# Unread TensorE products at the seams of a five-stage kernel, with three smaller edits beside them

## The chip, the cores and the metric

The kernel runs on one core of a Trainium2 chip. Its time is the device time of one execution in microseconds (us). Three runs of the kernel before are given, and one further execution was recorded by the profiler; every line of a profile below comes from that one.

## What is computed

The input x has 256 x 256 positions with 32 channels, in fp32. Four layers follow one another, and each adds its result to x:

```python
x = x + attention(_gn(x), ...)   # layer norm over channels, gate, values, projection
x = x + sobel(_gn(x))            # 3x3 mean, two 3x3 derivatives, sqrt(gx*gx + gy*gy + 1e-6)
x = x + sobel(_gn(x))
x = x + recurrence(_gn(x), ...)  # two recurrent layers, 256 steps, 256 sequences
```

`_gn` is a group norm: mean and variance over all positions, for 16 groups of two channels. In the attention the softmax runs over an axis of length one, so the values are merely multiplied by a sigmoid gate and projected. The recurrence has H = 128 hidden units, a normalisation of the four gates in each step, and biases and input weights that the kernel folds together with the last group norm ahead of the first step.

## The kernel before

The whole of x stays in SBUF as a tile of 128 partitions (four positions of one axis by 32 channels) by 64 blocks of 256 columns: `xa`, and a second one, `xb`. A pair is two blocks, 128 x 512; there are NST = 32 pairs. The engines run their own instruction queues in program order, and semaphores tie them together. Five stages follow one another:

1. Load (L163 to L184): x arrives by DMA, TensorE transposes it into PSUM, ScalarE copies it to `xa` (L183), VectorE takes statistics of each pair (L184).
2. Layer norm (L201 to L264). TensorE forms `pc`, the pairs with the group norm applied and their channel mean taken away (L238); ScalarE squares them, VectorE copies them to `xb`; TensorE gathers the variances into `pvar` (L228). ScalarE takes a root of `pvar` (L248), VectorE its reciprocal `rstd` (L249). Then for each pair TensorE spreads `rstd` over the channels into `pb` (L254, 32 rows of the array), VectorE multiplies `xb` by it (L261), and POOL applies `gamma4` and `beta4` (L262). `avg` and `spread`, constants that stage 2 needs, are made by POOL at its head (L204 to L213), when the load stage's SBUF has been released.
3. Attention (L268 to L332), in an order written out by hand. For each pair there are eight gate products `pg` and eight value products `pv` (L279, 32 rows each), sigmoids on ScalarE (L294), VectorE's products `o` (L297), a projection by sixteen matmuls (L303), whose result ScalarE moves out as `r` (L311); POOL adds it to `xa` (L313) and VectorE takes statistics (L316).
4. Sobel, twice (`sobel_layer`). A list of parts with due times, sorted, gives the order. Per pair, ScalarE normalizes the source twice, as `xp` and `xn` (L376); VectorE makes sums `u`, `pp`, `v`; POOL makes the two operands `dh` (L405) and `sh` (L401). TensorE applies the vertical part to them by centre and edge products (L412 or L422, and L452) into `pg1` and `pg0`. ScalarE squares (L458), VectorE adds (`ss`, L462), ScalarE takes the root (L466), VectorE adds the result to the source (L469) and takes statistics (L472). After each statistics part one entry of a list `between` is run. In Sobel 1 it holds the centring of the recurrent weights; in Sobel 2 it is empty.
5. Recurrence (`recurrence`), 256 steps by a plan with due times. The step's chain leads from the gate products `zz` (L763, L788, L793) over squares (L801), sums (L806), a power on POOL (L809), sigmoids and tanh to the new hidden state.

Between stages stands the group norm's seam. `group_norm` aggregates the statistics (`mv`, L139), averages over the group with a TensorE product of one column (`pm`, L141), forms the group variance on VectorE (`mean`, `d`, `q`), averages it with a second product (`pv`, L149), takes a root on ScalarE (`std`, L151), and makes `scale` and `bias`:

```python
nc.tensor.matmul(pm, lhsT=kt[:, K_GN, :], rhs=mv[:, 0:1], start=True, stop=True)
...
nc.vector.scalar_tensor_tensor(q, d, d, mv[:, 1:2], ALU.mult, ALU.add)
...
nc.scalar.activation(std, pv, AF.Sqrt, bias=gn_eps)
```

These steps wait for one another, so the engines are nearly idle there. In the text below seam 1 is the one between load and layer norm, seam 2 the middle of the layer norm (root and reciprocal) with its end, and seams 3, 4 and 5 stand before Sobel 1, Sobel 2 and the recurrence.

In the trace ScalarE has five ACT_TABLE_LOADs of 1283 ns: before the first copy of the load stage, before the first Sqrt (seam 1), before the first Sigmoid (attention), before the next Sqrt (seam 3) and before the next Sigmoid (recurrence). Each stands just ahead of the operation that needs it; Identity, copies and squares have none of their own.

`RecurrentWeights.products` (L607) forms, at seam 4, products of the recurrent weights: a transpose (`pl`), two products `pf` that VectorE adds to the biases `bc` (L617), and one, `pe`, that ScalarE copies in four pieces into `e4` (L625). `RecurrentWeights.finish` (L628) follows at seam 5; it writes `sb` from the group norm's result, forms two products `pg` with it (L641), which ScalarE copies to `fx`, and two small ones, `pk`. `RecurrentInputs` loads the inputs `xt` of the steps by DMA from `xa` and sets their rows of ones by POOL (L680).

Of the kernel before, what the change touches and what calls it, by code (L numbers as in the profile page):

```python
# [16 lines left out]
S = 256  # L17
T = 256
C = 32
# [39 lines left out]
def net_kernel(  # L59
# [71 lines left out]
    NST = NB // 2  # L131

# [3 lines left out]
    def group_norm(stats, psum):  # L136

        mv = small.tile([P, nc.vector.BN_AGGR_DIM], F32, name="mv")
        nc.vector.bn_aggr(mv, stats)  # L139
        pm = psum.tile([P, 1], F32, name="pm", tag="pm", bufs=1)  # L140
        nc.tensor.matmul(pm, lhsT=kt[:, K_GN, :], rhs=mv[:, 0:1], start=True, stop=True)  # L141
        mean = small.tile([P, 1], F32, name="mean")
        nc.vector.tensor_copy(mean, pm)
        d = small.tile([P, 1], F32, name="d")
        nc.vector.tensor_sub(d, mv[:, 0:1], mean)
        q = small.tile([P, 1], F32, name="q")
        nc.vector.scalar_tensor_tensor(q, d, d, mv[:, 1:2], ALU.mult, ALU.add)
        pv = psum.tile([P, 1], F32, name="pv", tag="pm", bufs=1)
        nc.tensor.matmul(pv, lhsT=kt[:, K_GN, :], rhs=q, start=True, stop=True)  # L149
        std = small.tile([P, 1], F32, name="std")  # L150
        nc.scalar.activation(std, pv, AF.Sqrt, bias=gn_eps)  # L151
        scale = small.tile([P, 1], F32, name="scale")
        nc.vector.reciprocal(scale, std)
        bias = small.tile([P, 1], F32, name="bias")
        nc.vector.scalar_tensor_tensor(bias, mean, -1.0, scale, ALU.mult, ALU.mult)
        return scale, bias

# [5 lines left out]
    with tc.tile_pool(name="nat", bufs=3) as natp, tc.tile_pool(  # L163
# [21 lines left out]
        gn = group_norm(stats, ps_in)  # L185
# [9 lines left out]
    KS = NST // 4  # L195
# [5 lines left out]
    with tc.tile_pool(name="ln", bufs=4) as lnp:  # L201


        avg = lnp.tile([P, KS, KS, J], F32, name="avg", bufs=1)  # L204
        nc.gpsimd.memset(avg, 0.0)
        for ks in range(KS):
            nc.gpsimd.tensor_copy(avg[:, ks, ks, :], kt[:, K_AVG, 0:P:C])
        spread = lnp.tile([P, KS * J, C], F32, name="spread", bufs=1)
        for g in range(4):
            rows = slice(g * C, (g + 1) * C)  # L210
            nc.gpsimd.tensor_copy(
                spread[rows], ident[rows, rows].unsqueeze(2).to_broadcast([C, KS * J, C])
            )  # L213
        rstd = lnp.tile([P, 2 * S], F32, name="rstd", bufs=1)
        with tc.tile_pool(name="ps_ln", bufs=6, space=PSUM) as ps_ln, tc.tile_pool(
# [32 lines left out]
            nc.scalar.activation(std, pvar, AF.Sqrt, bias=ln_eps)  # L248
            nc.vector.reciprocal(rstd, std)  # L249
        with tc.tile_pool(name="ps_sp", bufs=8, space=PSUM) as ps_sp:  # L250
            for k, g, ks in pairs:
                rows = slice(g * C, (g + 1) * C)
                pb = ps_sp.tile([P, 2 * S], F32, name="pb")
                nc.tensor.matmul(  # L254
                    pb,
                    lhsT=spread[rows, ks * J : (ks + 1) * J, :].rearrange("p j c -> p (j c)"),
                    rhs=rstd[rows, :],
                    start=True,
                    stop=True,
                )  # L260
                nc.vector.tensor_mul(pair(xb, k), pair(xb, k), pb)  # L261
                nc.gpsimd.tensor_scalar(  # L262
                    pair(xb, k), pair(xb, k), gamma4, beta4, ALU.mult, ALU.add
                )  # L264
# [4 lines left out]
    with tc.tile_pool(name="at", bufs=3) as atp, tc.tile_pool(  # L269
# [48 lines left out]
        with tc.manual_schedule():  # L318
            together((), [(0, j) for j in range(J)])
            together((), [(1, j) for j in range(2)])  # L320
            for i in range(NST):
# [5 lines left out]
                if i >= 1:  # L327
                    project(i - 1)
            for i in range(NST - 1, NST):
# [5 lines left out]
    with tc.tile_pool(name="ps_gn", bufs=1, space=PSUM) as ps_gn:  # L335
        gn = group_norm(stats, ps_gn)
# [8 lines left out]
    def sobel_layer(src, dst, scale, bias, between):  # L345
# [152 lines left out]
        with tc.manual_schedule():  # L498
            for _, k, part, args in todo:
                part(k, *args)  # L500
                if part is statistics and between:
                    between.pop(0)()
# [4 lines left out]
    with tc.tile_pool(name="ps_n", bufs=1, space=PSUM) as ps_n:  # L507
        gn = group_norm(stats, ps_n)
        rw.products(ps_n)
    stats = sobel_layer(xb, xa, *gn, [])  # L510
# [8 lines left out]
    with tc.tile_pool(name="ps_n", bufs=1, space=PSUM) as ps_n:  # L519
        gn = group_norm(stats, ps_n)  # L520
        weights = rw.finish(lw, ps_n, gn)
    with tc.If(plain > 0) as arms:
# [28 lines left out]
class RecurrentWeights:  # L551
# [31 lines left out]
    def centring(self):  # L583
# [21 lines left out]
        return [lambda p=out[i : i + 2]: [f() for f in p] for i in range(0, len(out), 2)]  # L605

    def products(self, psum):  # L607
        nc = self.nc
        pl = psum.tile([P, KX], F32, name="pl")
        nc.tensor.transpose(pl, self.lat, self.ident[:KX, :KX])  # L610
        nc.scalar.copy(self.latt, pl)
        for dst, src in ((self.lat4, self.latt[:, 0:C]), (self.wout4, self.wout)):
            nc.gpsimd.tensor_copy(dst, src.unsqueeze(1).to_broadcast([P, J, C]))
        for l in range(L):
            pf = psum.tile([KX, G], F32, name="pf", bufs=2)
# [3 lines left out]
        pe = psum.tile([P, C], F32, name="pe")  # L619
        nc.tensor.matmul(  # L620
            pe, lhsT=self.lat4.rearrange("p j c -> p (j c)"), rhs=self.wout, start=True, stop=True
        )
        for j in range(J):
            rows = slice(j * C, (j + 1) * C)
            nc.scalar.copy(self.e4[rows, rows], pe[rows, :])  # L625
        nc.gpsimd.tensor_add(self.e4, self.e4, self.ident)
# [31 lines left out]
class RecurrentInputs:  # L658
# [5 lines left out]
    def __init__(self, tc, ctx, xa):  # L664
# [12 lines left out]
        for i in range(self.NX):  # L677
            xt = kp.tile([P, self.XT, J, S], F32, name=f"xt{i}")
            for p in (0, X1):
                nc.gpsimd.memset(xt[p + C : p + KX], 1.0)  # L680
            self.xts.append(xt)
        for k in range(self.NX):
            self.load(k)

# [274 lines left out]
```

## Time and profile before

| | us |
|---|---|
| median of three runs | 2894.18 |
| the runs | 2893.24, 2903.16, 2894.18 |
| the profiled execution | 2892.63 |
| its span | 2890.8 |

| stretch of the profiled execution | us |
|---|---|
| load, up to its last statistics | 0 to 34.6 |
| seam 1, up to the first `pc` | 34.6 to 41.4 |
| layer norm, variances | 41.4 to 79.7 |
| seam 2 and spreading, up to the first `pg` | 79.7 to 105.4 |
| attention | 105.4 to 329.7 |
| seam 3, up to the first product of Sobel 1 | 329.7 to 339.4 |
| Sobel 1 | 339.4 to 480.5 |
| seam 4, up to the first product of Sobel 2 | 480.5 to 490.6 |
| Sobel 2 | 490.6 to 626.9 |
| seam 5, up to the first `zz` | 626.9 to 636.0 |
| recurrence | 636.0 to 2890.8 |

PE is TensorE's matmul queue and PEld its weight loads, DVE is VectorE, ACT ScalarE, POOL GpSimd, SP SyncE. One fp32 matmul appears as two passes, two rows of the trace. A timeline line gives start, duration, engine, line, operation, output<-inputs, shapes, and in brackets the idle time of the engine before it and what ended it. PEclk is the granted share of TensorE's clock. A line on waits gives the sum in us, how often, and the longest.

### The profile page before, as it was taken

To read this page: it belongs to the slowest core of one execution; us is meant where nothing else is said; L and a number is where in the kernel's file an instruction comes from. 1 tells how busy PE (TensorE), PEld (TensorE's weight loads), DVE (VectorE), ACT (ScalarE), POOL (GpSimd) and SP (SyncE) were. 2 spreads that over 40 slices of the span, in tenths; PEclk is the share of its full clock that TensorE was granted. 3 is DMA by queue.
4 is the path that set the end of the run, shared out by engine and by line. 5 is a ranking of instruction groups with operands and counts; after the bars stand their busy time and mean duration, and the time that the engine had idled before them with its cause. 6 is when DMAs were issued, how large, how long until landed. Compare 5 with 4: busy or idle time off the path is not lost.

```text
span 2890.8 us, 40872 instructions
## 1 busy us (share of the span) xinstructions
PE 2754.4 (95%) x9561; PEld 993.9 (34%) x9561; DVE 2422.5 (84%) x6507; ACT 2274.8 (79%) x6961; POOL 1934.2 (67%) x2586
## 2 busy tenths in 40 slices
PE   7899898989999999999999999999999999999997
PEld 4433333333333333333333333333333333333332
DVE  6788798978888888888888888888888888888886
ACT  5477676758888888888888888888888888888886
POOL 2311375657777777777777777777777777777775
PEclk9899999989999999999999999999999999999999
DMA  3000000000000000000000000000000000000000
GB/s 133 1 1 1 16 1 1 1 22 6 16 13 12 12 12 12 12 12 12 12 12 14 12 12 12 12 12 12 12 12 12 12 12 12 13 13 16 7 5 7
DMA packets 94354, 38.53 MB, mean 13 GB/s; under 512 B 74852, under 2 KB 91269, under 8 KB 94104
## 3 DMA queue, kind: packets, MB, share of 16 engines
q1 hardware_dynamic: 93156, 34.67, 5.3%
q8 instruction: 79, 1.29, 0.2%
q14 instruction: 171, 1.40, 0.2%
q10 hardware_dynamic: 148, 0.86, 0.1%
q0 software_dynamic: 800, 0.30, 0.0%
HBM read 10.63 MB, written 8.39 MB: 7 GB/s over the span
## 4 chain that ended last, share of the span: by engine, by line
PE 44%; DVE 32%; POOL 12%; issue 7%; ACT 2%; POOLq 0%; DVEq 0%; ACTq 0%
DVE ve L806 14%; POOL rs L809 11%; PE zz L793 11%; DVE c L852 7%; PE zz L788 6%; PE zz L763 5%; DVE zn L773 4%; PE pv L279 4%; PE pg L452 4%; PE pg L412 3%; DVE c L844 3%; PE pt L864 3%; PE pg L303 2%; PE px L883 2%; PE pg L279 1%
## 5 line engine op out<-in xcount | busy, mean ns | idle before, releaser
L809 POOL TENSOR_TENSOR rs<-ve,mhalf 128x4 f32<-128x4 f32 x1024 | 1040.3, 1016 | 252.0 <-DVE ve L806 225.5
L793 PE MATMUL zz<-wc,hT 128*128 128x512 f32 x2040 | 962.2, 594 | 1.2 <-DVE hT L869 1.2
L801 ACT ACTIVATE sq<-zz 128x512 f32<-128x512 f32 x1024 | 605.4, 591 | 245.7 <-PE zz L793 240.3
L806 DVE TENSOR_REDUCE ve<-sq 128x4 f32<-128x516 f32 x1024 | 694.4, 678 | 9.9 <-ACT sq L801 9.5
L848 POOL TENSOR_TENSOR fc<-ga,c 128x128 f32<-128x128 f32 x1020 | 464.8, 456 | 333.4 <-ACT ga L837 313.3
L782 ACT ACTIVATE ga<-zz,rs 128x128 f32<-128x128 f32 x2048 | 585.0, 371 | 4.6 <-POOL rs L809 1.1
L763 PE MATMUL zz<-fx,xt 33*128 33x512 f32 x2048 | 585.2, 643 | 3.3 <-issue 1.9
L788 PE MATMUL zz<-wc,hT 128*128 128x512 f32 x1024 | 525.3, 595 | 0.0
L793 PEld LDWEIGHTS zz<-wc,hT 128*128 128x128 f32 x2040 | 361.0, 197 | 262.6 <-DVE hT L869 201.6
L844 DVE TENSOR_TENSOR c<-ga 128x128 f32<-128x128 f32 x1024 | 307.5, 300 | 156.3 <-ACT ga L782 98.3
L773 DVE TENSOR_TENSOR zn<-zz,rs 128x256 f32<-128x256 f32 x1024 | 386.2, 419 | 54.8 <-POOL rs L809 20.4
L864 PEld LDWEIGHTS pt<-ident,h 128*128 128x128 f32 x1024 | 142.3, 139 | 797.9 <-DVE h L859 748.9
L864 PE MATMUL pt<-ident,h 128*128 128x128 f32 x1024 | 323.7, 316 | 67.4 <-DVE h L859 40.8
L856 ACT ACTIVATE th<-c 128x128 f32<-128x128 f32 x1024 | 310.4, 303 | 79.6 <-DVE c L852 59.8
L852 DVE TENSOR_TENSOR c<-c,fc 128x128 f32<-128x128 f32 x1020 | 368.8, 362 | 3.1 <-POOL fc L848 2.0
L859 DVE TENSOR_TENSOR h<-ga,th 128x128 f32<-128x128 f32 x1024 | 290.2, 283 | 0.8 <-ACT th L856 0.8
L763 PEld LDWEIGHTS zz<-fx,xt 33*128 33x128 f32 x2048 | 156.6, 185 | 348.2 <-PE zz L793 309.0
L869 DVE COPY hT<-pt 128x128 f32<-128x128 f32 x512 | 147.5, 288 | 111.5 <-PE pt L864 111.5
L837 ACT ACTIVATE ga<-zn 128x256 f32<-128x256 f32 x512 | 208.7, 408 | 3.9 <-DVE zn L773 3.9
L297 DVE TENSOR_TENSOR o<-pv,sg 128x512 f32<-128x512 f32 x256 | 158.0, 679 | 46.5 <-PE pg L279 37.7
L874 POOL TENSOR_TENSOR hs<-hT,hT 128x256 f32<-128x256 f32 x256 | 186.0, 726 | 1.7 <-ACT hT L869 1.7
L788 PEld LDWEIGHTS zz<-wc,hT 128*128 128x128 f32 x1024 | 183.3, 219 | 2.3 <-issue 2.3
(143 smaller groups left out, 2745.6 us busy)
## 6 DMA issues: line engine op xcount, KB each, us to landing
xt<-xa SPq DMA_DIRECT2D x256, 64.0 KB, 2.0
nat<-in_x_dram SPq DMA_DIRECT2D x16, 512.0 KB, 7.1
out_dram<-st SPq DMA_DIRECT2D x256, 32.0 KB, 1.7
wc<-in_L_conv_W_cell_dram SPq DMA_DIRECT2D x2, 512.0 KB, 4.5
kt<-in_consts_dram ACTq DMA_DIRECT2D x1, 832.0 KB, 5.9
wv<-in_L_conv_Wv_dram POOLq DMA_DIRECT2D x4, 32.0 KB, 5.0
wg<-in_L_conv_Wg_dram POOLq DMA_DIRECT2D x4, 32.0 KB, 6.0
gamma<-in_L_conv_ln_gamma_dram POOLq DMA_DIRECT2D x4, 0.1 KB, 6.3
```

What stands on the lines that cost most here:

```text
L763: nc.tensor.matmul(zz, lhsT=x, rhs=fx[rows, l, :], start=True, stop=l == 0 and t == 0)
L773: nc.vector.tensor_mul(four(get("zn"))[:, g, :], four(get("zz"))[:, g, :], get("rs")[:, g].unsqueeze(2).to_broadcast([P, 2, H]),)
L782: nc.scalar.activation(gates(get("ga"), g), gates(x, g), func, scale=scale)
L788: nc.tensor.matmul(get("zz"), lhsT=v["hT", 0, t][:, seqs], rhs=wc[:, l, 0, :], start=False, stop=t == 0)
L793: nc.tensor.matmul(get("zz"), lhsT=v["hT", l, t - 1][:, seqs], rhs=wc[:, l, 1, :], start=False, stop=True,)
L801: nc.scalar.activation(sqs[l, h][:, :, 0:H], four(get("zz")), AF.Square, scale=float(H**-0.5))
L806: nc.vector.tensor_reduce(ve, sqs[l, h], AX.X, ALU.add)
L809: nc.gpsimd.tensor_tensor(rs, get("ve"), inputs.mhalf, ALU.pow)
L844: nc.vector.tensor_mul(c, gates(get("ga"), 0), gates(get("ga"), 3))
L848: nc.gpsimd.tensor_mul(fc, gates(get("ga"), 1), get("c"))
L852: nc.vector.tensor_add(c, c, get("fc"))
L864: nc.tensor.transpose(pt[:, 0:P], get("h"), ident)
```

## The change

Five things are done. `busy` puts unread products (the identity by a 256-column slice, written to a PSUM tile that nobody reads) on TensorE: in `group_norm` before `pm`, two between `pm` and `pv`, and some after `pv`; nine behind the layer norm's root; ten behind the last `pb`. `table` puts a one-element activation of a given function ahead of the place that needs it, so that the table is loaded there. Every second pair of `gamma4`/`beta4` goes from POOL to ScalarE. The weight products move from seam 4 into the `between` list of Sobel 2, where they write to a buffer of `pg1`. POOL's copies for `avg` and `spread` move ahead of the load stage, and POOL's rows of ones behind `finish` in the program.

What the queues hold after it: the products before `pm` stand behind the last ScalarE copy of L183 (seam 1), the last `r` of L311 (seam 3), or the last residual of L469 (seams 4 and 5). The nine wait for the root of L248, the ten for the multiplication of the 25th pair in L261. The Sqrt table of seam 3 is loaded between the last two `r`. In `finish`, `pg` now stands before `pk`. POOL's rows of ones stand at the same place of its queue as before, and no DMA moves on its queue. In the recurrence's steps each engine's instructions and their order are the same, but for the table load ahead of the first sigmoid.

```diff
+    def table(func, after):
+        t = small.tile([P, 1], F32, name="table")
+        nc.scalar.activation(t, after, func, scale=0.0, bias=one)
+
+    def busy(psum, n, rhs=None):
+        junk = psum.tile([P, S], F32, name="junk", tag="junk", bufs=1)
+        for _ in range(n):
+            nc.tensor.matmul(
+                junk, lhsT=ident, rhs=kt[:, 0:2, :] if rhs is None else rhs, start=True, stop=True
+            )
...
-    def group_norm(stats, psum):
+    def group_norm(stats, psum, before, after, rhs=None):
         nc.vector.bn_aggr(mv, stats)
+        busy(psum, before, rhs)
         pm = psum.tile([P, 1], F32, name="pm", tag="pm", bufs=1)
         nc.tensor.matmul(pm, lhsT=kt[:, K_GN, :], rhs=mv[:, 0:1], start=True, stop=True)
+        busy(psum, 2, rhs)
...
         nc.tensor.matmul(pv, lhsT=kt[:, K_GN, :], rhs=q, start=True, stop=True)
+        busy(psum, after, rhs)
...
-        gn = group_norm(stats, ps_in)
+        table(AF.Sqrt, xa[:, NB - 1, 0:1])
+        gn = group_norm(stats, ps_in, 3, 2, xa[:, NB - 1, :])
...
             nc.scalar.activation(std, pvar, AF.Sqrt, bias=ln_eps)
+            table(AF.Sigmoid, std[:, 0:1])
             nc.vector.reciprocal(rstd, std)
+            for _ in range(9):
+                nc.tensor.matmul(
+                    pvar[:, 0:S], lhsT=ident, rhs=kt[:, 0:2, :], start=True, stop=True
+                )
...
-                nc.gpsimd.tensor_scalar(
-                    pair(xb, k), pair(xb, k), gamma4, beta4, ALU.mult, ALU.add
+                if i % 2:
+                    nc.scalar.activation(
+                        pair(xb, k), pair(xb, k), AF.Identity, scale=gamma4, bias=beta4
+                    )
+                else:
+                    nc.gpsimd.tensor_scalar(
+                        pair(xb, k), pair(xb, k), gamma4, beta4, ALU.mult, ALU.add
+                    )
+            junk = ps_sp.tile([P, 2 * S], F32, name="pb")
+            for _ in range(10):
+                nc.tensor.matmul(
+                    junk[:, 0:S], lhsT=ident, rhs=kt[:, 0:2, :], start=True, stop=True
                 )
...
                     project(i - 1)
+            table(AF.Sqrt, one)
             for i in range(NST - 1, NST):
                 project(i)
...
-        gn = group_norm(stats, ps_gn)
+        gn = group_norm(stats, ps_gn, 7, 12)
...
                 if part is statistics and between:
-                    between.pop(0)()
+                    between.pop(0)(lambda: flat(ps_s.tile([P, 2, S], F32, name="pg1")))
...
-        gn = group_norm(stats, ps_n)
-        rw.products(ps_n)
-    stats = sobel_layer(xb, xa, *gn, [])
+        gn = group_norm(stats, ps_n, 6, 12)
+    stats = sobel_layer(xb, xa, *gn, rw.products())
...
-        gn = group_norm(stats, ps_n)
+        gn = group_norm(stats, ps_n, 9, 3)
+        table(AF.Sigmoid, gn[0])
         weights = rw.finish(lw, ps_n, gn)
+        inputs.ones()
...
+        def turn(ps):
+            pl = ps()[:, 0:KX]
+            nc.tensor.transpose(pl, self.lat, self.ident[:KX, :KX])
+            nc.scalar.copy(self.latt, pl)
...
+        def biases(ps, l):
+            pf = ps()[0:KX, :]
             nc.tensor.matmul(pf, lhsT=self.latt, rhs=self.wc[:, l, 0, :], start=True, stop=True)
             nc.vector.tensor_add(self.bc[:, l, :], self.bc[:, l, :], pf)
...
+        return [
+            turn,
+            repeat,
+            lambda ps: biases(ps, 0),
+            lambda ps: biases(ps, 1),
+            output,
+        ]
```

The lines of `avg` and `spread` move unchanged from the layer norm to a place ahead of the load stage, into the pool of constants. `repeat` holds POOL's two broadcast copies, and `output` the product `pe` with its four copies and POOL's addition.

## The prediction

> **What bounds the kernel now.** (Lines are those of the kernel before.) I read the page first, then the stretches between the clock's changes, then the timeline at each seam between stages.
>
> ```profile
> span 2890.8 us, 40872 instructions
> ...
> PEclk9899999989999999999999999999999999999999
> ...
> PE 44%; DVE 32%; POOL 12%; issue 7%; ACT 2%; POOLq 0%; DVEq 0%; ACTq 0%
> ```
>
> The recurrence fills the span from 636 us on, about 8.7 us for each of 256 steps, at full clock. The instructions of its steps, and their order on every engine, stay as they are, so it prices at 0, and what can be won lies in the first 650 us. There the granted clock drops in places. By stretches (us, then busy us of PE, PEld, DVE, ACT, POOL, the clock, DMA):
>
> ```profile
> 37.69:44.52 6.83, 4.27 (x8) 2.52 (x9) 1.46 (x6) 2.23 (x3) 0.39 (x1) 0.50 0.01 1
> 78.65:82.07 3.42, 1.06 (x12) 0.15 (x5) 2.21 (x2) 0.69 (x1) 0.00 (x0) 1.00 0.00 0
> 82.07:88.89 6.82, 4.88 (x22) 2.73 (x24) 4.66 (x6) 0.00 (x0) 1.88 (x3) 0.50 0.00 1
> 92.31:95.72 3.41, 3.41 (x13) 1.68 (x12) 3.41 (x7) 0.00 (x0) 3.41 (x5) 1.00 0.00 0
> 95.72:116.20 20.48, 15.74 (x57) 10.76 (x58) 12.10 (x21) 6.60 (x11) 15.27 (x21) 0.50 0.00 1
> 331.24:344.89 13.65, 6.11 (x18) 3.80 (x18) 7.51 (x14) 6.50 (x11) 7.08 (x7) 0.50 0.18 66
> 474.60:478.01 3.41, 2.30 (x11) 0.64 (x9) 1.92 (x4) 1.87 (x3) 0.14 (x2) 1.00 0.00 0
> 478.01:481.43 3.42, 1.26 (x3) 0.28 (x3) 2.60 (x4) 0.88 (x2) 0.29 (x1) 1.00 0.00 0
> 481.43:495.08 13.65, 7.91 (x19) 4.64 (x21) 8.64 (x17) 5.90 (x14) 6.54 (x6) 0.50 0.00 0
> 628.20:652.09 23.89, 18.94 (x29) 6.66 (x30) 7.93 (x27) 7.66 (x18) 9.54 (x8) 0.50 0.19 47
> 652.09:2860.00 2207.91, 2146.87 (x6711) 749.72 (x6710) 1893.43 (x5641) 1836.10 (x6149) 1645.14 (x2280) 1.00 0.06 12
> ```
>
> Six half-clock spells, all multiples of 3.41 us. A stretch of 3.41 us with TensorE 31% or 37% busy (78.65, 478.01) is followed by a drop, one with 67% (474.60) is not. The 32-row products of L254 lose the clock although PE looks full (92.31).
>
> **The Trainium skill.** "TensorE: Matmul & The Clock Gate", section on the HAM clock gate: a free-running 3.4 us window halves the clock after an idle window and restores it after a busy one. The trace agrees in length and in ratio: weight loads of successive 512-wide passes start 0.43 us apart at 75 us and 0.85 at 43 us. "ScalarE: Activation LUTs", "What ACT_TABLE_LOAD costs", gives 1283 ns for a load, and a drain beside it; the trace has 1283 ns and no drain (std starts 0.01 us after). "SBUF — State Buffer", "Who interferes with whom": a VectorE operation with two SBUF inputs and a GpSimd one that reads SBUF block each other. That is d and q here, behind POOL's copies of L211 (0.68 and 1.05 us; 0.16 and 0.22 at the next seam, where no copy runs):
>
> ```profile
> 36.32 0.68 DVE L145 TENSOR_TENSOR d<-mv,mean 128x1 f32<-128x1 f32 x1
> 37.03 1.05 DVE L147 SCALAR_TENSOR_TENSOR q<-d,mv 128x1 f32<-128x1 f32 x1
> ...
> 38.82 1.28 ACT L151 ACT_TABLE_LOAD   x1 [5.26 <-PE pv L149]
> 40.11 0.26 ACT L151 ACTIVATE std<-pv,gn_eps 128x1 f32<-128x1 f32 x1
> ```
>
> **Price of one unread product.** 128x256 in fp32 is two passes of half the width above: 0.43 us at full clock, 0.85 at half. TensorE keeps its order, so a product delays all that stands behind it.
>
> **Seam 1 (load to layer norm).** The POOL copies move up to about 20 us, so q takes 0.22 and pv could start at 36.8 instead of 38.14. The two products behind pm (35.70) hold PE to about 36.95: pv 1.2 us earlier. The table load (1.28) now runs behind the last copy of L183, at 33.6. From pv at 36.95, std at 37.4, bias by 38.1; the two products behind pv end then too, so pcb starts at 38.15 and the first pc at 38.6 instead of 41.42: 2.8 us. Three products from 33.6 and these four make 3.0 us of work in 5 us, about half of each window, above the 37% that lost the clock, so I take it as held: the pc stream then lacks 3.1 us at half clock, worth 1.55. It is the chain to 79.7 (PE full, DVE 24 of 38 us). **-4.3**; -1.5 if the clock still drops.
>
> **Seam 2 (inside the layer norm).** (Times of before; what seam 1 gave comes off all of them.) Nine products from 80.6 end at 84.5 (3.9 us) and their result is waited for; the reciprocal ends at 83.95, so pb starts 0.65 later than now (84.01), but at full clock: first result 1.05 us after it instead of 2.09. Net -0.4. Then VectorE alone sets the pace, 32 x 0.60 us, to 104.9. POOL's half of gamma/beta on ACT (16 x 0.80, the row of L376) fits into that; POOL ended at 110.99, but nobody waited for its last tiles: 0. The ten products need the bank of the 25th pair, free at 100.65. The clock will have dropped again by then (L254's stream fell to half at 95.7). At 0.85 until one full window passes (about 3.9 us on average), then 0.43: done at 106.9. pg, which waits for that and for VectorE, starts at 107.0 instead of 105.44: **+1.6**. What follows it is shorter:
>
> ```profile
> 107.56 1.28 ACT L294 ACT_TABLE_LOAD   x1 [26.99 <-PE pg L279]
> ...
> 113.39 2.48 DVE L297 TENSOR_TENSOR o<-pv,sg 128x512 f32<-128x512 f32 x4 [8.05 <-PE pv L279]
> ```
>
> From pg to the first o were 7.95 us. Without the table load, with four pg done in 1.1, a sigmoid (0.6), the next two pg and a pv at full clock, about 3.4: o at 110.4, -3.0. VectorE then waits once more for 0.75 (after four o, PE still at half clock), of which I count half: **-3.4**; -5.5 with the ten at full clock, -1 with all ten at half.
>
> **Seam 3 (attention to Sobel 1).** The Sqrt table (1.28 + 0.26) is put between the last two r of L311, where ACT is idle for only 1.1 us: r, POOL's add and the statistics come 0.45 later. It saves 1.3 behind pv. Seven products from 328.1 end at 331.1, before mv (331.2). The two behind pm delay pv by 0.2; pv itself is 0.25 shorter. xp starts 0.9 earlier. Twelve products then fill 5.2 us, up to dh (338.4). The gap before the first is 1.4 us, so the clock holds, and the first two pairs take half. VectorE, full in Sobel, had this wait:
>
> ```profile
> DVE ss L462 <- ACT sq L458: 3.0, 1, 3.0
> ```
>
> It shrinks to 1.1, since POOL's sh and dh (1.0 us each) then lead: with the 0.9, **-2.8**; -3.5 if it goes further, +1 if the clock drops.
>
> **Seam 4 (Sobel 1 to 2).** The weight products leave: pf stood before pv (1.1 us), the four e copies before xp (0.5). But the six products wait for the last residual of L469 (479.78) and take 2.6 us at full clock, and mv is ready at 481.6. PE idles 2.95 us before them, so in about two cases of three a window empties and they run partly at half: 4.2 us. pm comes 0.9 or 2.5 late, xp 0.9 early or 0.6 late. The start of Sobel 2 at full clock gives 1.5 either way. Mean **-1.5**, from -2.4 to +1. The products move into Sobel 2, where VectorE has no idle time: two additions of 0.67 us, **+1.3**; ACT, POOL and PE have room there. A held pg1 bank may cost up to 1.5 more, and half may hide: 0.5 to 3.
>
> **Seam 5 (Sobel 2 to recurrence).** The same, with nine:
>
> ```profile
> 625.44 0.69 DVE L469 TENSOR_TENSOR xa<-xb,pg 128x512 f32<-128x512 f32 x1 [0.76 <-ACT pg L466]
> ...
> 626.89 1.02 DVE L139 BATCH_NORM_AGGREGATE mv<-stats 128x2 f32<-128x192 f32 x1
> 628.05 0.43 PE L141 MATMUL pm<-mv,kt 128*128 128x1 f32 x2 [4.81 <-DVE mv L139]
> ```
>
> From 626.2 they last 3.9 to 5.5 us: pm at 630.1 to 631.7, **2.0 to 3.6 late**. Then three products behind pv are over before VectorE has sb. The two pg at full clock take 1.7 instead of 3.7 us, and pk follows instead of leading: first zz at 635.8 to 637.4 (636.00). Its own passes give 1.0 back. The table load was hidden under L809 and is hidden again. The first products have 33 rows, so the clock drops again soon after. POOL's ones keep their place in its queue; no DMA on SP or POOL's queue moves: 0. About **-0.1**, from -2.5 to +2.5.
>
> **Sum.** -4.3 - 3.4 - 2.8 - 1.5 + 1.3 - 0.1 = -10.8 us. The profiled execution took 2892.6 (span 2890.8 and 1.8 around it), which becomes 2881.8; the median of the runs lies 1.6 above it: **2883.4 us**.
>
> **Rivals.** (a) The clock is held at every seam, the ten products and seams 4 and 5 included: -4.3 - 5.5 - 3.5 - 2.4 + 0.5 - 2.5 = -17.7, 2876.5. Against it: L254's stream, and 2.95 us of idle PE before seams 4 and 5. (b) The products give back what they win: pm late in seams 4 and 5, the ten before pg, bank stalls in Sobel 2, and only table loads, POOL's copies and part of the clock remain: -1.5 - 2 - 1.8 + 1 + 2 + 1 = -1.3, 2893. For it: three of five groups start too late to end before their release. (c) Slower: unread products do not hold or lift the clock, so that the change does not do what it says, and they stand in the way at 0.85 us. Seam 2: 9 and 10 of them put pg 8.5 later, less the table 7.2. Seam 3: pm 3.1 late, pv another 1.3, and twelve more end 7.8 after dh was ready before. Seam 4: 7.4 and 1.3. Seam 5: 8. Total +31, 2925; it decides for slower once three of these four seams run so. Against it: a stream of L238 lifted the clock at 44.5.
>
> **Numbers.** 0.5% is 14.5 us, about what a measurement of this kernel can tell from no change. The forecast 0.60, (a) 0.15, (b) 0.20, (c) 0.05. Past -14.5 lie two thirds of (a) and a twelfth of the forecast (its better ends together): faster 0.15, slower 0.05, same 0.80. The range runs from the edge of (a), 2876, to (b), 2893; left out are (c), half of (b) and a tail of (a).
>
> **What will tell.** Right: full clock from 14 us to about 92, and through 331 to 345; no table load behind any pv; the first o about 29.8 us behind the start of the reciprocal (32.8 now); mv to pm longer at seams 4 and 5 than the 0.06 and 0.14 us now. Wrong: half clock during the twelve products, a wait on VectorE inside Sobel 2, or a step of the recurrence that is not 8.7 us.

## The result and the profile after

| | before | after |
|---|---|---|
| median of 13 runs, us | 2895.58 | 2891.75 |
| lowest to highest, us | 2893.24 to 2903.16 | 2885.46 to 2897.56 |
| profiled execution (span), us | 2892.63 (2890.8) | 2886.19 (2884.4) |

The ratio of after to before is 0.9982 [0.9973, 0.9992]: 0.2% faster, where 10.8 us (0.37%) were forecast. The medians differ by 3.8 us, the profiled executions by 6.4.

The page of the kernel after answers to the three lines shown of before:

```profile
span 2884.4 us, 41191 instructions
...
PEclk9999999999999999999999999999999999999998
...
DVE 32%; PE 26%; POOL 12%; issue 7%; ACT 2%; POOLq 0%; DVEq 0%; ACTq 0%
```

Up to the end of the recurrence the clock's tenths show no dip any more. The 8 in the last slice is the end of the recurrence: its last steps run at half clock, here from 2869.8 us on (14.6 us), in the kernel before from 2877.6 us on (13.3 us). In the last chain TensorE's share is 26% instead of 44%, with VectorE and POOL as before. That is no gain: this chain can be followed back only to 630.4 us, inside the recurrence, that of before to 41.4 us, through all stages, so it says nothing of the seams. The stretches between the clock's changes are the view that matters (us, then busy us of PE, PEld, DVE, ACT, POOL, the clock, DMA share, GB/s):

```profile
23.08:26.49 3.41, 3.37 (x17) 2.96 (x16) 2.50 (x4) 2.34 (x4) 0.99 (x1) 0.50 1.04 396
36.00:42.80 6.80, 6.11 (x23) 3.87 (x23) 3.28 (x10) 2.29 (x5) 0.00 (x0) 1.00 0.00 1
84.53:87.94 3.41, 3.41 (x13) 1.62 (x12) 3.41 (x7) 2.26 (x4) 2.22 (x3) 1.00 0.01 2
87.94:101.59 13.65, 13.65 (x40) 10.11 (x39) 13.65 (x23) 9.19 (x12) 8.86 (x12) 0.50 0.00 1
331.40:345.00 13.60, 13.36 (x48) 5.25 (x46) 10.81 (x17) 8.42 (x16) 9.99 (x8) 1.00 0.00 1
627.23:630.65 3.42, 2.59 (x9) 1.19 (x8) 0.52 (x3) 1.18 (x2) 0.00 (x0) 1.00 0.48 108
630.65:644.31 13.66, 10.19 (x14) 2.91 (x14) 6.42 (x17) 4.39 (x13) 3.67 (x5) 0.50 0.03 6
644.31:2860.00 2215.69, 2153.00 (x6733) 750.59 (x6733) 1901.51 (x5657) 1843.85 (x6167) 1650.80 (x2286) 1.00 0.06 11
```

Three half-clock spells ahead of the recurrence's steady part where before had six, 30.7 us instead of 85.3 in all. Seam 1 and the start of Sobel 1 run at full clock. The 32-row products of the spreading still lose the clock (84.53, then 13.65 at half), and so do the first products of the recurrence.

By stages, worked out from the start and end times in each trace. The half-clock spells ahead of the last steps all last a multiple of 3.41 us, so the clock is taken to change at the edges of windows of that length; the phase is where these edges fall in the kernel. "Other phase" is the profile of experiment E14, which has the same instructions as the kernel after up to the start of the recurrence, but met the clock's windows at other places. "End of attention" is from VectorE's last `o` to `mv`. "Load" runs to the first `mv`; it varied by 34.4 to 36.2 us over all the profiles, with no order by kernel.

| stage | before, us | after, us | difference | forecast | other phase, difference |
|---|---|---|---|---|---|
| load | 34.63 | 35.60 | +1.0 | 0 | 0.0 |
| seam 1 and variances | 45.08 | 40.64 | -4.4 | -4.3 | -4.4 |
| root, spreading, attention | 245.27 | 243.41 | -1.9 | -3.4 | -0.7 |
| end of attention, seam 3, Sobel 1 | 155.55 | 152.88 | -2.7 | -2.8 | -1.0 |
| seam 4 to the first `ss` of Sobel 2 | 16.73 | 14.20 | -2.5 | -1.5 | -1.0 |
| Sobel 2 | 129.61 | 132.40 | +2.8 | +1.3 | +2.8 |
| seam 5 to the first `zz` | 9.11 | 9.22 | +0.1 | -0.1 | +1.8 |
| recurrence | 2254.84 | 2256.04 | +1.2 | 0 | +0.5 |
| sum | 2890.84 | 2884.40 | -6.4 | -10.8 | -2.0 |

Seam 1 in the timeline of the kernel after (start, duration, engine, line, operation; the line numbers are those of each run's own kernel):

```profile
34.61 1.28 ACT L137 ACT_TABLE_LOAD   x1
...
37.29 0.16 DVE L161 TENSOR_TENSOR d<-mv,mean 128x1 f32<-128x1 f32 x1
37.48 0.22 DVE L163 SCALAR_TENSOR_TENSOR q<-d,mv 128x1 f32<-128x1 f32 x1
...
38.18 0.26 ACT L168 ACTIVATE std<-pv,gn_eps 128x1 f32<-128x1 f32 x1 [1.98 <-PE pv L165]
```

`d` and `q` take 0.16 and 0.22 us instead of 0.68 and 1.05, as the copies no longer run beside them (POOL is idle from 36.00 to 42.80), and the table load is over before `pv`. This seam went as forecast.

Between spreading and attention it did not. L296 holds the ten products, L313 `pg`, L328 the sigmoid, L331 `o`:

```profile
99.54 5.28 PE L296 MATMUL pb<-kt,ident 128*128 128x256 f32 x19
...
104.92 1.14 PE L313 MATMUL pg<-xb,wg 32*128 32x512 f32 x8
106.11 3.04 ACT L328 ACTIVATE sg<-pg 128x512 f32<-128x512 f32 x6 [3.58 <-PE pg L313]
...
108.84 4.28 DVE L331 TENSOR_TENSOR o<-pv,sg 128x512 f32<-128x512 f32 x7 [7.15 <-PE pv L313]
```

VectorE's last multiplication ends at 101.68; `pg` starts 3.2 us later, behind the ten. VectorE idles 7.15 us instead of 8.05.

VectorE's waits inside Sobel 1 and then inside Sobel 2 (sum, how often, longest):

```profile
DVE ss L497 <- ACT sq L493: 1.2, 1, 1.2
```

```profile
DVE u L418 <- ACT xn L411: 1.9, 3, 0.7
```

The wait at the start of Sobel 1 fell from 3.0 to 1.2. In Sobel 2, `u` waits three times for `xn`. Before it did so once:

```profile
DVE u L383 <- ACT xn L376: 0.7, 1, 0.7
```

Seam 5, from the last residual (L504) over the unread products (L143) to `pm`:

```profile
617.69 0.69 DVE L504 TENSOR_TENSOR xa<-xb,pg 128x512 f32<-128x512 f32 x1 [0.76 <-ACT pg L501]
...
618.52 4.12 PE L143 MATMUL junk<-kt,ident 128*128 128x256 f32 x18 [3.02 <-DVE xa L504]
619.14 1.02 DVE L153 BATCH_NORM_AGGREGATE mv<-stats 128x2 f32<-128x192 f32 x1
622.48 0.28 PE L156 MATMUL pm<-mv,kt 128*128 128x1 f32 x2
```

`mv` is ready at 620.16 and `pm` starts at 622.48: 2.3 us, where before it was 0.14.

### The profile page after: what moved, and what is told of

Its sections match the earlier page's. It is cut to its first block, busy times and chain, and to the rows that moved or that the text cites. A ratio compares the mean times of both kernels' runs of the same rounds, so it can differ in the third digit from the quotient of the medians.

```text
span 2884.4 us, 41191 instructions
## 1 busy us (share of the span) xinstructions
PE 2773.8 (96%) x9723; PEld 1014.4 (35%) x9723; DVE 2424.1 (84%) x6507; ACT 2291.9 (79%) x6981; POOL 1923.9 (67%) x2571
## 4 chain that ended last, share of the span: by engine, by line
DVE 32%; PE 26%; POOL 12%; issue 7%; ACT 2%; POOLq 0%; DVEq 0%; ACTq 0%
DVE ve L863 14%; POOL rs L866 11%; PE zz L850 11%; DVE c L909 8%; PE zz L845 5%; DVE zn L830 5%; PE zz L820 4%; DVE c L901 3%; PE pt L921 3%; PE px L940 2%; DVE h L916 1%; ACT fin L948 1%; PE px L937 1%; DVE st L951 1%; ACT ga L898 0%
## 5 line engine op out<-in xcount | busy, mean ns | idle before, releaser
L331 DVE TENSOR_TENSOR o<-pv,sg 128x512 f32<-128x512 f32 x256 | 158.1, 681 | 44.9 <-PE pg L313 37.7
```

## Experiments

**Theories.** T1, fixed costs: what the products win is lost again at the ten, in Sobel 2 and at the products that wait for the last residual. T2, phase: the clock's window runs free, so the same kernel loses the clock at different places from run to run, and the profile shows one case only. The expectations call their own alternatives Theory A and Theory B. Edits are on the kernel after unless said otherwise. Each ratio is to the kernel before, run beside it. The kernel before had medians of 2894.95 to 2897.54 us in these comparisons, so runs that were not made side by side are compared by their ratios.

**E1, no unread product at all.**

```diff
-        for _ in range(n):          # busy
+        for _ in range(0):
-            for _ in range(9): ...  # behind the root
-            for _ in range(10): ... # behind the last pb
```

> The changed kernel without any unread product (those in group_norm, the nine and the ten); tables, POOL's halves and copies and the weight products stay. Theory A (the products hold the clock where they can start at once, and that is worth it): seam 1 loses 1.5 us, the start of Sobel 1 1.7, the start of Sobel 2 2.0, while pm in seams 4 and 5 comes 0.8 and 2.0 earlier and pg in the attention 3 us earlier but cold; in all 3 to 5 us slower than the changed kernel, about level with the kernel before. Theory B (they give back what they win, the gain is the table loads and POOL's copies): within 1 us of the changed kernel, or faster.

2893.14 us, 0.9981 [0.9975, 0.9988]. Without any unread product the kernel is as fast as with all 81 of them; the two intervals leave room for about 3 us either way. The mean clock is 0.982 to 0.983 here and 0.987 to 0.993 in the runs of the kernel after: the products hold the clock, and over the runs this brings no time that can be seen.

**E2, without the ten. E3, weight products back at the seam. E4, none ahead of `pm` at seams 4 and 5.**

```diff
-            for _ in range(10): ...                                     # E2
-    stats = sobel_layer(xb, xa, *gn, rw.products())                     # E3
+        for part, ... in zip(rw.products(), tiles): part(...)           # at the seam
+    stats = sobel_layer(xb, xa, *gn, [])
-        gn = group_norm(stats, ps_n, 6, 12)                             # E4
+        gn = group_norm(stats, ps_n, 0, 12)
-        gn = group_norm(stats, ps_n, 9, 3)
+        gn = group_norm(stats, ps_n, 0, 3)
```

> The changed kernel without the ten products at the end of the layer norm. Theory A (they start at half clock, end about 3 us after the last multiplication and only swap a wait for a warm start): pg starts 3.1 us earlier, the first o comes 6.6 us after it instead of 4.0, so the time stays within 1 us of the changed kernel. Theory B (the prediction's step): 1.7 us slower than the changed kernel.

> The changed kernel with the weight products back at seam 4, beside its unread products. Theory A (in Sobel 2 they cost two additions and two waits on a late ScalarE, 2.8 us together): Sobel 2 is 2.8 us shorter, the seam 1 to 1.5 longer, in all 1 to 2 us faster than the changed kernel. Theory B (the prediction's step, 1.3 in Sobel 2 against 1.6 at the seam): within 0.5 us.

> The changed kernel without the products that stand before pm in seams 4 and 5 (6 and 9 become 0). Theory A (they wait for the last residual and then stand in pm's way): pm follows mv within 0.5 us at both seams, 0.8 and 2.0 us earlier than in the changed kernel's profile; the clock falls at both, which costs up to 2 us at the start of Sobel 2; in all 1 to 3 us faster than the changed kernel. Theory B (holding the clock is worth the wait): 1 to 2 us slower.

E2 2890.10 us, 0.9975 [0.9965, 0.9984]; E3 2889.32, 0.9973 [0.9964, 0.9982]; E4 2892.64, 0.9983 [0.9977, 0.9990]. All three intervals overlap that of the kernel after; the stages are clearer. In E2 `pg` starts at once and VectorE waits less, although the clock is at half:

```profile
101.59 2.09 PE L308 MATMUL pg<-xb,wg 32*128 32x512 f32 x8 [2.76 <-issue]
...
108.24 1.89 DVE L326 TENSOR_TENSOR o<-pv,sg 128x512 f32<-128x512 f32 x3 [6.76 <-PE pv L308]
```

VectorE waits 6.76 us without the ten, and 7.15 to 8.54 in seven profiles with them. The ten cost 0.4 to 1.8 us; a start of attention at full clock is worth less than the wait for it. E3 puts Sobel 2 back at 129.65 us and leaves `u` with one wait:

```profile
DVE u L418 <- ACT xn L411: 0.7, 1, 0.7
```

So the weight products cost 2.75 us there. Two additions take 1.2, and 1.2 more are waits on `xn`. One of these waits is shown here: `xn` stands on ScalarE behind the four copies of `e4` (L672; L418 is the `u` that waited):

```profile
510.83 0.72 ACT L672 COPY e<-pg 32x32 f32<-32x32 f32 x4
```

```profile
515.63 0.69 DVE L418 TENSOR_TENSOR u<-xn,xp 128x510 f32<-128x510 f32 x1 [0.45 <-ACT xn L411]
```

In E4 `pm` follows `mv` within 0.06 us at both seams, but the clock is gone at both: the first `ss` of Sobel 2 comes 11.75 us after `bias` instead of 9.99, and seam 5 takes 10.76 us instead of 9.22.

**E5, fill ahead of the seam instead of behind the last residual. E6, ten products spread over the spreading. E7, weight products split over Sobel 1, the seam and Sobel 2.**

```diff
+            fill = flat(ps_s.tile([P, 2, S], F32, name="pg1"))           # E5, end of sobel_layer
+            for _ in range(9): ...                                      #     and 0 ahead of pm at seams 4, 5
+                if i % 4 == 3:                                          # E6, instead of the ten
+                    for _ in range(2): ...
+    stats = sobel_layer(xa, xb, *gn, rw.centring() + weight[0:2])       # E7
+        for part in weight[2:4]: part(...)                              #     behind pv of seam 4
+        busy(ps_n, 8)
+    stats = sobel_layer(xb, xa, *gn, weight[4:])
```

> The changed kernel, but at the end of each Sobel layer nine unread products go straight behind the last edge products, into the pg1 buffer whose turn it is (free since the residual before the last two), and none wait for the last residual. Theory A (lateness of the products, not the idea, costs at seams 4 and 5): pm follows mv within 0.5 us at both seams and the clock stays full there; mv to bias 3.4 to 3.7 us at seam 4, mv to the first zz about 7.3 at seam 5; the first ss of Sobel 2 10 us after bias; 2 to 4 us faster than the changed kernel. Theory B (a held clock is worth nothing there): within 1 us of the changed kernel without those products.

> The changed kernel without the ten products behind the spreading; instead two unread products stand behind every fourth product of rstd, in a PSUM bank of their own (the spreading keeps seven). Theory A (the 32-row products load the array too little to hold the clock, and the ten come too late): the clock stays full through the spreading, its 32 multiplications still take 19.2 us, and the first o follows the last of them by 4.0 to 4.5 us instead of 7.2 to 8.5; 3 to 4 us faster than the changed kernel. Theory B (the attention's start waits for ScalarE or VectorE anyway): within 1 us.

> The changed kernel, with the weight products split: transpose and copies in Sobel 1's list, the two bias products right behind pv at seam 4 with eight unread products behind them instead of twelve (an order written out), only pe with its copies in Sobel 2. Theory A (in Sobel 2 the two additions and the waits they bring cost 2.8 us, at the seam VectorE has time for them): Sobel 2 is back at 129.6 to 130, seam 4 and the start of Sobel 2 no longer than in the changed kernel; 2 to 3 us faster. Theory B (the additions or their products delay the start of Sobel 2 as much): within 1 us.

E5 2892.97 us, 0.9988 [0.9980, 0.9997]: not the gain expected. The clock is held over both seams in its profile, but `pm` still starts 1.2 us after `mv` is ready, since three unread products that stand behind it in the program came ahead of it in TensorE's queue. Its runs fall into two heaps, 2886 to 2889 at a mean clock of 0.990 to 0.992 and 2892 to 2895 at 0.988 to 0.989. E6 2889.37, 0.9978 [0.9970, 0.9985]: the clock holds through the spreading to 101.87 and drops just as attention starts, so `o` comes at 6.76 as without any. E7 2889.36, 0.9977 [0.9967, 0.9987]: Sobel 2 at 130.45 and Sobel 1 at 135.14 (134.38), so 1.2 us of the 2.8 are saved, net.

**E8, all three together,** with no product ahead of `pm`, seam 4 in a written-out order, and unread products at the recurrence's start:

```diff
+        busy(ps_n, 3)                    # behind the weights of the recurrence
+    at(-1e4, fill, 8)                    # ahead of the second projection
+    for when, n in ((8.2, 3), (12.3, 2), (16.6, 2), (20.5, 2)):
+        at(when, fill, n)                # nine, 8 to 21 us after the first zz
```

> The three together, and unread products at the start of the recurrence as well: three behind the folded weights, eight behind the first zz, and eleven spread over the first two steps. Theory A: 3 and 3.5 and 2.5 us from the three, and if the clock is held through the first steps another 2 to 3: 9 to 12 us faster than the changed kernel, 14 to 17 than the kernel before. Theory B (the products delay the first steps): the recurrence takes longer than the 2253 to 2258 us seen so far.

2882.27 us (2880.57 to 2882.80 in five runs), 0.9950 [0.9936, 0.9964]: faster than both kernels, and the runs lie close. (Nine products are spread over the first steps, where the expectation says eleven.)

**E9, no unread product, and weight products at the seam** (E1 and E3 together). **E10, unread products only where they end in time** (E2 and E3, none ahead of `pm` at seams 4 and 5). **E11, E8 without the products at the recurrence's start. E12, the kernel after again.**

> No unread product anywhere, and the weight products back between Sobel 1 and Sobel 2 as they were before; what is left of the change is the table loads, POOL's copies moved to the start, the ones moved behind the seam and half of the scale on ScalarE. If the weight products cost 2.8 us inside Sobel 2 and about 1 us at the seam: Sobel 2 takes 129.6 us instead of 132.4, the seam 4.7 instead of 3.7, about 2891.4, ratio about 0.9975, faster than the kernel without unread products by 1.8. If the additions hide in Sobel 2 as half hidden (1.3): no difference from that kernel, 2893, 0.9981.

> Unread products only where the trace lets them end before their release: seam 1, the nine behind the reciprocal, seam 3, behind pm and pv of seams 4 and 5; none of the ten, none that wait for the last residual; weight products at the seam. If the fixed costs are what ate the gain (0.4 to 1.8 for the ten, 2.8 in Sobel 2, 0.9 to 2.4 at seam 4 and 2.0 to 3.5 at seam 5): about 2886, ratio about 0.9965, with seam 4 at 4.7 and pm within 0.2 us of mv at both seams. If the phase of the clock's window decides: seams 4 and 5 lose the clock more often without these products, Sobel 2 starts 2 us slower and the recurrence 1 to 2, and it stays at 2889 to 2891, 0.9975 to 0.998.

> As the run of all parts together, without the unread products at the start of the recurrence. If the recurrence's first steps profit from the clock: 2.0 to 2.5 us more, 2884.6, ratio 0.9958, and the stage of the recurrence at 2256 to 2257. If those products only stand beside work that has time to spare: 2882.3, 0.9950, and 2254.

> The changed kernel once more, for a second profile. If the phase of the clock's window sets its spread of 12 us: another set of half-clock spells, the seams of Sobel 1 and 2 at 5.9 to 6.8 and 10.8 to 12 us where the clock is lost (4.21 and 9.22 in the first profile), the end of attention at 6.6 to 6.8 where it drops there (5.15), times that rise by 2 us for each thousandth that the mean clock falls, median 2889 to 2893. If it is something else (transfers, for one): the same three spells at the same places, and the spread in stages without a spell.

E9 2895.87 us, 0.9997 [0.9988, 1.0005]; E10 2890.24, 0.9977 [0.9968, 0.9986]; E11 2890.57, 0.9970 [0.9959, 0.9981]; E12 2888.89, 0.9976 [0.9965, 0.9987]. E9 and E10 miss what T1 gave them, and E11 loses about 6 us against E8 by the ratios, not 2. In the profiles of all three the recurrence is long: the stage takes 2261.67, 2260.32 and 2261.22 us (2254.84 before, 2253.96 in E8). The clock returns 29.8, 27.9 and 29.7 us after the first `zz`; before it returned after 16.1, in E8 after 5.4. The time from the first `zz` to the 41st `ve` (the sums of the step, L806 in the kernel before, four in each step) covers about ten steps; it is 100.6, 99.3 and 100.7 us in the three, 94.2 in the kernel before and 93.3 in E8. So the loss stands at the start. The stretch at half clock in E9, and the PE timeline inside it:

```profile
624.88:662.42 37.54, 31.93 (x49) 10.59 (x49) 14.13 (x45) 13.76 (x38) 14.47 (x13) 0.50 0.13 30
```

```profile
647.29 0.42 PE L915 MATMUL pt<-ident,h 128*128 128x128 f32 x1
648.10 2.08 PE L844 MATMUL zz<-wc,hT 128*128 128x512 f32 x2 [0.38 <-DVE hT L920]
650.10 2.08 PE L814 MATMUL zz<-fx,xt 33*128 33x512 f32 x4
652.11 2.07 PE L839 MATMUL zz<-wc,hT 128*128 128x512 f32 x2
653.98 0.42 PE L915 MATMUL pt<-ident,h 128*128 128x128 f32 x1
```

From `pt` to `pt` it is 6.69 us at half clock (4.32 across the clock's return in the kernel before), and two windows last 6.83. The windows stay at nearly the same place of this cycle, and each cycle brings 2.08 us of 33-row products. In the last five windows of the spell PE is 89 to 100% busy, and only the fifth brings the clock back; this fits a rise missed again and again, but that is not shown, and what separates the window that lifts it from its neighbours was not found: one with 3.03 us of 128-row products in 3.41 lifted it before, one with 3.04 did not in E9.

E12, the same instructions as the kernel after, supports T2: another set of spells (319.88 to 323.29 is new), and the end of attention at 6.71 us instead of 5.15. Seams 4 and 5 kept the clock again.

**E13, E14, E15: the products of the recurrence's start alone** (the three `at` and `for` lines of E8), on the kernel before, the kernel after and E9.

> The kernel before with unread products at the start of the recurrence only (eight ahead of the second projection, nine spread over the first five steps). If the late rise of the clock there sets the time: it rises within 10 us of the first product, the recurrence takes about 2254, median about 2891.5, ratio 0.998, and the runs lie within 4 us (9 us for the kernel before). If the seams make the spread: 2896 to 2897.5, ratio 1.000, spread as before. If the products stand in the recurrence's way: 2899 or more.

> The changed kernel with the same products at the start of the recurrence. If the late rise sets its median: 2885, ratio 0.9960, runs within 6 us, the recurrence at about 2254 (2256.04 and 2254.68 in its two profiles). If the phase at the seams does: 2889 to 2891.5, 0.9975 to 0.998, spread still 10 us.

> Table loads, POOL's copies and half of the scale on ScalarE, no unread product except those at the start of the recurrence. If the late rise ate what these edits win: the recurrence falls from 2261.67 to about 2254, median 2888, ratio 0.997. If the edits win nothing at all: 2895 to 2896, 0.9995.

E13 2895.96 us, 0.9996 [0.9988, 1.0005]: no gain. E14 2890.53, 0.9977 [0.9968, 0.9985]: not the 2885 expected. E15 2891.49, 0.9984 [0.9977, 0.9992]: about 4 us less than E9 by the ratios, and the clock is back 9.3 us after the first `zz`:

```profile
624.86:641.92 17.06, 14.79 (x29) 8.20 (x30) 4.53 (x17) 5.13 (x11) 8.43 (x6) 0.50 0.29 66
```

So in E9 the late rise ate what table loads and copies win (their first `zz` is at 632.64 us, 3.4 earlier than before), and the products get most of it back: 96.0 us to the 41st `ve` for 100.6. In E13 they only shorten a spell that had ended after 16.1 us, to 8.6, and cost more than they save: 95.8 us for 94.2. E14 shows that the recurrence's start is not what sets the median of the kernel after. Its profile has 2255.36 there and loses 4.9 us elsewhere: at the end of attention 6.80 (5.15), seam 4 5.78 (4.21), seam 5 10.91 (9.22). The stretches of its windows:

```profile
314.60:318.00 3.40, 3.40 (x12) 1.17 (x8) 3.40 (x6) 0.96 (x2) 0.86 (x1) 1.00 0.00 0
318.00:321.41 3.41, 3.41 (x17) 0.79 (x20) 2.53 (x5) 0.00 (x0) 0.00 (x0) 0.50 0.00 0
...
471.60:475.01 3.41, 1.18 (x6) 1.08 (x7) 2.58 (x4) 0.69 (x1) 0.00 (x0) 1.00 0.00 0
475.01:478.42 3.41, 3.41 (x11) 2.78 (x10) 0.48 (x2) 0.00 (x0) 0.00 (x0) 0.50 0.00 0
...
618.37:621.78 3.41, 0.61 (x2) 0.00 (x0) 1.96 (x3) 1.68 (x3) 2.55 (x7) 1.00 0.32 72
621.78:625.20 3.42, 3.20 (x8) 2.60 (x9) 1.79 (x3) 0.00 (x0) 3.31 (x3) 0.50 0.44 101
```

And the same places in the first profile of the kernel after, at its own windows:

```profile
470.23:473.64 3.41, 1.72 (x8) 1.57 (x9) 2.50 (x4) 0.69 (x1) 0.00 (x0) 1.00 0.00 0
...
617.00:620.41 3.41, 1.89 (x9) 1.71 (x10) 2.40 (x3) 0.65 (x1) 3.30 (x3) 1.00 0.45 103
```

In E14 the 3.0 us of idle PE before the unread products fall into one window (busy 35% and 18% of it) and the clock drops; in the first profile they are cut in two by a window's edge (50% and 55%) and it holds. The products then run at half clock and last longer at just that place: at seam 4 of E14 they hold PE from 473.83 to beyond 477.9, and `pm` starts at 477.94 with `mv` ready at 475.47.

**E16, E8 again.**

> The kernel with all parts, once more. If it is free of the phase at the seams and at the recurrence's start: 2880 to 2884 in all runs, ratio 0.995, one short spell after the first zz. If the first five runs met one good phase: runs from 2881 to 2891, median about 2887, ratio 0.997, and where it is slow the recurrence takes over 2256 or the end of attention 6.8.

2883.29 us (2880.43 to 2884.97 in five runs), 0.9955 [0.9942, 0.9969]: the gain is there again. The one spell near the first `zz` is 3.41 us long, the end of attention 5.15, seam 4 3.30, seam 5 8.88, as in E8.

## Why the prediction was wrong

The direction held, and the products hold the clock as forecast. That they win the time in most runs did not hold: E1 has none and is as fast. Rival (b), "the products give back what they win", at 2893, came nearer than the forecast, and it named what took the gain: `pm` late, the ten ahead of `pg`, stalls in Sobel 2 (not on a bank, but on ScalarE). Rival (a) fails at the ten (-1.9 in that stage, not -5.5) and at seam 5 (+0.1, not -2.5, with the clock held). Rival (c) fails because the products do hold the clock; its terms as listed add up to 36.1 us, not to 31.

The profiles differ by 6.4 us, not 10.8; and the kernel after lies further above its profile (2891.75 - 2886.19 = 5.6) than the kernel before does (2895.58 - 2892.63 = 2.95). 6.4 - 5.6 + 2.95 = 3.8 us, what was measured. So of the 7.0 us missing, 4.4 are missing in the profiles too, and 2.6 appear only over the runs. Of the 4.4, 2.2 are net terms of the sum that were mis-sized, seam 2 and Sobel 2 above all; the other 2.2 are the load (+1.0) and the recurrence (+1.2), for which no cause in the change was found. Another 1.4 of the forecast's distance is the median of before, 2894.18 of three runs and 2895.58 of thirteen.

- **Seam 1, -4.3: right** (-4.4). Its own fallback for a dropped clock, -1.5, fits too: E1, without the products, keeps 1.7.
- **Seam 2, -3.4: wrong, the step "first o -3.0".** The ten ended 3.1 us after VectorE's last multiplication, not 2.0. From `pg` to `o` it was then 3.9 us (3.4 forecast), and without the ten 6.7, but with no wait ahead of it: the wait took what the full clock gave. Only the table (1.3) was a gain; against E2 the ten were a loss of 0.4 to 1.8. From the start of the reciprocal to the first `o` it is 31.8 us, not the 29.8 that were to show the prediction right.
- **Seam 3, -2.8: right in the first profile** (-2.7): the end of attention +0.4, `bias` 1.5 earlier, `ss` 2.0 sooner, and +0.4 inside Sobel 1 that was not forecast. What the forecast did not have is the drop at the end of attention, +1.6 in other phases: 32-row products fill the window 314.60:318.00.
- **Seam 4, -1.5:** -2.5 and -1.0 in the two phases. The calculation for both cases, `pm` 0.9 or 2.5 us late, came out as 1.03 and 2.47 from the end of `mv` (0.06 before). This was the right way to price it.
- **Sobel 2, +1.3: +2.8.** The failed step is "ACT, POOL and PE have room there". ScalarE is 74% busy in that stage, but four copies in a row push a root and an `xn` back, and VectorE, which has no slack, waits for them. Of the extra time 1.2 us are these waits, the prediction's own sign of being wrong. An average of busy time does not tell how late one instruction may come.
- **Seam 5, -0.1:** +0.1 in the first profile, +1.8 in the phase of E14, inside the -2.5 to +2.5 given.
- **Recurrence, 0: +1.2,** but not from the clock at its start. It returned after 16.0 us (16.1 before), and the steps up to the 41st `ve` took 93.9 us (94.2). Most of the +1.2 stands in the steps at full clock behind them, up to the 40th `ve` from the end: 2056.6 us (2055.4), and 2055.0 to 2056.8 over all profiles; why is open. The prediction saw the clock drop at the start and put it at nothing. Without products there, that costs little where it returns after 15 to 17 us (93.4 to 94.9 us to the 41st `ve`), and 5 to 7 us more where it takes 28 to 30 (99.3 to 100.7), which hid the gain of the table loads in E9.

On the phase, the Trainium skill ("TensorE: Matmul & The Clock Gate", Part 1, the HAM clock gate) warns that the window is free-running, so that the same kernel shows different numbers of slow products from run to run. The runs of one kernel agree with the page: 2886.09 us at a mean clock of 0.992 and 2894.86 at 0.988 in E5. Over the 13 runs of the kernel after a fitted line gives 2.2 us for each thousandth of the mean clock (correlation -0.95). An unread product that starts after an idle stretch does not always prevent the drop; in the windows shown for E14 and the kernel after, where the window's edge fell decided it.

The prediction priced seams 4 and 5 in both phases, and its "two cases of three" was close: of the seven profiles with the same unread products there (the kernel after, E2, E3, E6, E7, E12, E14) four lost the clock at seam 4 and five at seam 5. It did not price the end of attention, lost in five of the seven profiles with the ten (the kernel after, E3, E4, E5, E7, E12, E14). The first profile of the kernel after lost none of the three. At the 1.6, 1.6 and 1.7 us that a loss costs in E14, this makes a mean of about 3.3 us above that profile, an estimate from these profiles, near the 2.6 that appear only over the runs. That the phase is all of the 2.6 is not shown: most of these profiles are of other kernels, and the slower of the two profiles of the kernel after is a run of 2888.25.

How much each part of E8 brings by itself is also open beyond E11: without the recurrence's products it is about 6 us slower by the ratios (0.9970 for 0.9950).

## What to carry to other kernels

Price a filler (an unread product) by when it can start. One that waits for the last result of the stage before delays the next stage, and most where the clock is lost (`pm` 1.0 or 2.5 us late at seam 4); with fillers ahead of that wait, and none that waits, the clock held and the delay was gone (seam 4 in E8, 3.30 us instead of 4.21 to 5.78). Before counting on a clock that is held at one place, list all places where the same window can lose it and what each costs in both phases; what counts is the median over phases. Here the kernel after and E2 to E7 stayed 0.1 to 0.3% below the kernel before, and only E8, with fillers ahead of the waits and at the recurrence's start too, reached 0.5%. Work moved into a stage whose bound engine has no slack costs the waits behind its small copies as well as its own instructions on that engine.

## What the hardware showed unexpectedly

- The recurrence's first steps stay at half clock with PE 85% busy (31.93 us of the 37.54 in E9): the clock came back only 29.8 us after the first `zz`, in other profiles after 5.0 to 29.7. At the other end, the last 12.6 to 14.6 us of every profile run at half clock again.
- Unread products of 128 rows cost 0.43 us each at full clock and held it at seam 1 and the start of Sobel 1 (331.40:345.00); but 32-row products with PE at 100% lost it: in the spreading in every profile without fillers between them (84.53:87.94 in the kernel after), and, depending on the phase, at the end of attention (314.60:318.00 in E14).
- A mean clock higher by 0.007 (0.983 to 0.990 in the median run) came with no change of time (E1 and the kernel after, ratios 0.9981 and 0.9982).
